# Which queue loads x in the first stage of a graph-convolution kernel: GpSimd's for every row group with known degrees

## The chip, the cores and the metric

The kernel runs on one core of a Trainium2 chip. The metric is the device time of one execution in microseconds; lower is better.

## What is computed

Inputs are `x` (8 x 4096 x 256, float32), `adj` (4096 x 4096, float32, almost all zeros outside a few dense rows and columns) and `W` (256 x 256). The reference, cut to what matters:

```python
HW = einsum('bnf,fo->bno', x, W)
A_norm = relu((adj + adj.T) * 0.5)
D = sum(A_norm, axis=1)
d = where(D > 0, D ** -0.5, 0)
L_norm = eye(N) - d[:, None] * A_norm * d[None, :]
y = relu(einsum('nm,bmo->bno', L_norm, HW))
out = layernorm(x + y, axis=-1)
```

## The kernel before

The work has two stages that follow each other. The first makes the symmetric matrix and the scaled features and puts both into device memory; the second gathers the non-zero parts of the matrix and multiplies.

**First stage.** `adj` is cut into 8 x 8 blocks of 512 x 512. The loop runs over rows of blocks i = 0 to 7 and, in each, over j = i to 7. One step (i, j) does this:

- SP's queue loads block (i, j) and, off the diagonal, block (j, i) (`load_adj`, line 485, 1 MB each, into a pool of 4 buffers).
- `symmetrise`: TensorE transposes one block by pieces of 128 x 128 (line 495), VectorE adds the other block to it into a `sym` tile (line 499, pool of 3 buffers). Off the diagonal both blocks are done, so a step has 32 transposes and 8 additions.
- Work "beside" it: `multiply` (line 564), the product of an already finished row group with the first 128 columns of the matrix (its "strip"), 8 matmuls; and `form` (lines 575 to 624) for one row group m of 128 nodes.
- `keep`: ScalarE halves and clips (line 503), VectorE sums each 32 columns (line 506, into a pool of 3 `sums` buffers), GpSimd marks which sums are positive (`uses`, line 507), VectorE adds up row sums (line 511), and ScalarE's queue stores the tile to `a_dram` (line 512, 1 MB).

After a row of blocks its degrees are complete: GpSimd raises them to the power -1/2 (`r`, line 526), and corrected diagonal blocks are stored to `a_dram` from GpSimd's queue (line 538).

**`form(m, known, alone)`** loads the 8 x 128 x 256 part of x that belongs to row group m, in two halves of 512 KB (`xin`, a pool of 3 buffers), transposes it on TensorE (line 595, 16 pieces; 8 for each half), copies it out with ScalarE (line 596) and multiplies by W (line 606, 32 matmuls). If the degrees of the group are known, ScalarE scales the result (line 616), stores it to `g_dram` (line 621) and calls `fetch(m)`, which loads the strip for the later `multiply`. If they are not, the result is held in on-chip memory and scaled later (`release`); these are the last ten groups, 22 to 31. The groups with known degrees are 0 to 21. Steps with i = 1 to 3 form groups 0 to 11 (and, in row 1, the held groups 30 and 31); steps with i = 4 to 7 form groups 12 to 21.

The two loads of `form` go one of two ways. With `alone` false they are issued on SP's queue (line 588), among the adj loads. With `alone` true they go through `load` (line 554) on GpSimd's queue, where each is placed behind the load issued by `load` before it; the strips go through the same function, so x loads and strips form one sequence there. The call that chooses is line 711.

Each engine executes its instructions in order, and a DMA that waits for its buffer keeps what is behind it on that engine's queue waiting. A scheduler fixes the order on each queue when the program is built. On GpSimd's queue stand, in the first stage, the `uses` operations, the powers `r`, the diagonal copies and stores, the strips, short memsets of constants for the second stage (lines 214, 215 and 221, some 45 after each `uses` up to about 138 us), and the x loads with `alone` true.

**Second stage.** GpSimd issues indirect loads of matrix rows (line 951) and of features (line 959), TensorE multiplies them (line 1166), and ScalarE, VectorE and SP's queue evict, normalise and store.

Of the kernel before, what the change touches and what calls it, by code (L numbers as in the profile page):

```python
# [67 lines left out]
def kernel(  # L68
# [401 lines left out]
    with (  # L470
# [12 lines left out]
        def load_adj(i, j):  # L483
            t = blocks_pool.tile([P, A, S], F32, tag="adj", name=f"adj_{i}_{j}")
            nc.sync.dma_start(
                t,
                adj[i * S : (i + 1) * S, j * S : (j + 1) * S].rearrange("(a p) s -> p a s", p=P),
            )
            return t

        def symmetrise(i, j, tij, tji, sym):
            for a in range(A):
                pt = psum.tile([P, S], F32, tag="b0", name=f"tr_{i}_{j}_{a}")
                for c in range(A):
                    ins = nc.tensor.transpose(  # L495
                        pt[:, c * P : (c + 1) * P], tji[:, c, a * P : (a + 1) * P], ident
                    )
                done_pe.append(ins.ins)
                nc.vector.tensor_add(sym[:, a, :], pt, tij[:, a, :])  # L499
                yield  # L500
# [50 lines left out]
        def load(t, source):  # L551

            with tc.issue_after(loads[-1]) if loads else nullcontext():
                loads.append(nc.gpsimd.dma_start(t, source).ins)

        def fetch(m):

            t = strips.tile([P, P], F32, tag="strip", name=f"strip_{m}")
            load(t, a_dram[m * P : (m + 1) * P, :P])
            return t  # L560

        def multiply(m, g, strip):
            for c in range(G // S):
                nc.tensor.matmul(  # L564
                    lead[c],
                    lhsT=strip,
                    rhs=g[:, c * S : (c + 1) * S],
                    start=not done,
                    stop=len(done) == NB - 1,
                    skip_group_check=True,  # L570
                )
                yield
            done.append(m)

        def form(m, known, alone=False):

            H = B // 2  # L580
            xin = []
            for h in range(2):
                t = xpool.tile([P, H, F], F32, tag="xin", name=f"xin_{m}_{h}", bufs=3)
                source = x[h * H : (h + 1) * H, m * P : (m + 1) * P, :].rearrange("b p f -> p b f")
                if alone:
                    load(t, source)
                else:
                    nc.sync.dma_start(t, source)
                xin.append(t)
            xt = xpool.tile([P, B, FC, P], F32, tag="xt", name=f"xt_{m}", bufs=1)  # L590
            for b in range(0, B, 2):
                pt = psum.tile([P, 2, FC, P], F32, tag="b0", name=f"xtr_{m}_{b}")
                for k in range(2):
                    for c in range(FC):
                        nc.tensor.transpose(pt[:, k, c, :], xin[b // H][:, b % H + k, c * P : (c + 1) * P], ident)  # L595
                nc.scalar.copy(xt[:, b : b + 2], pt)  # L596
                yield
            if known:
                g = xpool.tile([P, G], F32, tag="g", name=f"gt_{m}")
            else:  # L600
                g = hpool[m].tile([P, G], F32, name=f"held_{m}")
            for b in range(0, B, 2):
                pg = psum.tile([P, 2 * FO], F32, tag="b0", name=f"pg_{m}_{b}")
                for k in range(2):
                    for c in range(FC):
                        ins = nc.tensor.matmul(  # L606
                            pg[:, k * FO : (k + 1) * FO],
                            lhsT=xt[:, b + k, c, :],
                            rhs=w_sb[:, c, :],
                            start=(c == 0),  # L610
                            stop=(c == FC - 1),
                        )
                done_pe.append(ins.ins)
                to = g[:, b * FO : (b + 2) * FO]
                if known:
                    nc.scalar.mul(to, pg, r[:, m : m + 1])
                else:
                    nc.scalar.copy(to, pg)
                yield
            if known:  # L620
                nc.scalar.dma_start(g_dram[m * P : (m + 1) * P, :], g)
                waiting.append((m, g, fetch(m)))
            else:
                held[m] = g
# [12 lines left out]
        def release_all(i):  # L637
            for m in range(i * A, (i + 1) * A):
                if m in held:
                    release(m)  # L640
            lower_diagonal(i, diags.pop(i))
# [3 lines left out]
        known, early = [], list(range(NB - HOLD, NB))  # L645

        def quota(i, j):

            if i in (2, 3) and j == i:
                return 0  # L650
            return int(j > i or i > 3)
# [3 lines left out]
        def run_due(flush=False):  # L655
            for d in due:
                d[0] -= 1
            while due and (flush or due[0][0] <= 0):
                _, fn, args = due.pop(0)
                fn(*args)  # L660
# [37 lines left out]
        for i in range(NS):  # L698
            diag = stat1.tile([P, A, P], F32, tag="diag", name=f"diag_{i}")
            for j in range(i, NS):  # L700
                tij = load_adj(i, j)
                tji = load_adj(j, i) if j > i else tij
                parts = [(i, j, tij, tji)] + ([(j, i, tji, tij)] if j > i else [])
                parts = [(p, spool.tile([P, A, S], F32, tag="sym", name=f"sym_{p[0]}_{p[1]}")) for p in parts]
                beside = [multiply(*args) for args in waiting]
                waiting.clear()
                products = len(beside)

                for _ in range(quota(i, j)):
                    if known:  # L710
                        beside.append(form(known.pop(0), True, i >= 4))
                    elif early:
                        beside.append(form(early.pop(0), False))
                for p, sym in parts:
                    for _ in symmetrise(*p, sym):
                        pass
                if i == NS - 1:


                    release_all(i - 1)  # L720
                    beside = beside[products:] + beside[:products]
                for n, b in enumerate(beside):
                    with tc.issue_after(done_pe[-1]) if i == NS - 1 and n < 2 else nullcontext():
                        for _ in b:
                            pass
                for (rows, cols, _, _), sym in parts:
                    keep(rows, cols, sym, diag)
                    run_due()
            degrees(i)
            diags[i] = diag  # L730
            if i != NS - 2:
                release_all(i)
            known += range(i * A, min((i + 1) * A, NB - HOLD))
            if i in (1, 2, 3, 4):
                u = SEQ[i - 1]
                at = 4 if i == 4 else 1
                gap = 2 if i == 1 else 1
                due += [[at, patterns, (u,)], [at + 1, count_place, (u,)]]
                due += [[at + 1 + (k + 1) * gap, more, (u,)] for k in range(3)]
                if i < 4:  # L740
                    due.append([at + 2 + 3 * gap, count_place_rest, (u,)])
            if i in (2, 4):
                u = SEQ[i // 2 - 1]
                at = 4 if i == 2 else 0
                pieces = spread_early(u)
                due += [[at + k, next, (pieces, None)] for k in (1, 2, 3, 3, 4)]
                due.append([at + 5, collect_index, (u,)])
            due.sort(key=lambda d: d[0])
# [579 lines left out]
```

## Time and profile before

| What | us |
|---|---|
| median of 3 runs | 1491.0 (1484.07 to 1491.29) |
| profiled execution, its time | 1490.8 |
| profiled execution, its span | 1488.3 |
| PE busy, of the span | 1381.5 (93%) |
| VectorE busy | 1042.9 (70%) |
| GpSimd busy | 761.4 (51%) |
| ScalarE busy | 360.8 (24%) |

The span runs from the first to the last instruction of the profiled execution; 2.5 us of its time lie around it. In the page's queue list, q1 is SP's queue, q10 is ScalarE's and q0 is GpSimd's:

```profile
q0 software_dynamic: 55200, 282.68, 49.1%
q1 hardware_dynamic: 93472, 126.89, 24.7%
q10 hardware_dynamic: 67872, 130.32, 23.1%
```

The columns are packets, MB, and the time that their packets took as a share of 16 DMA engines over the span. The x loads of the first stage and their neighbours in the list of DMA issues (queue, count, KB each, median us to landing):

```profile
adj<-in_adj_dram SPq DMA_DIRECT2D x64, 1024.0 KB, 10.2
a_dram<-sym ACTq DMA_DIRECT2D x64, 1024.0 KB, 8.9
...
xin<-in_x_dram SPq DMA_DIRECT2D x44, 512.0 KB, 11.9
...
xin<-in_x_dram POOLq DMA_DIRECT2D x20, 512.0 KB
```

A line such as "PE tr L495 <- DVE sym L499: 11.2, 10, 4.0" in the list of waits says that PE's instruction of line 495 was let go by VectorE's of line 499, for 11.2 us in total in 10 cases, of which the longest took 4.0 us. PEld is TensorE's weight load; SPq is SP's queue, which only issues DMAs. The granted clock is the share of full speed at which TensorE was allowed to run. The DMA share is the busy share of the core's 16 DMA engines; as packets overlap, it can stand a little above 1.

### The profile page before, as it was taken

The numbers are of one execution on the slowest core, as the hardware profiler recorded it, in microseconds if no ns is written. First come the engines' busy times: TensorE is split into PE (matmuls) and PEld (weight loads), VectorE is DVE, ScalarE is ACT, GpSimd is POOL, SyncE is SP. The second block draws the span as 40 slices with busy tenths as digits, with TensorE's granted clock in tenths as the row PEclk, the third lists the DMA queues.
The fourth block names the chain that finished last, engine by engine and source line by source line (L and its number), as shares of the span: only waits on it lengthen the run. The fifth ranks groups of instructions, "written<-read, shape, count | busy, mean of one in ns | idle before, by whom it ended". The sixth has DMA issues, their size and how long they took to land.

```text
span 1488.3 us, 29574 instructions
## 1 busy us (share of the span) xinstructions
PE 1381.5 (93%) x10960; PEld 749.5 (50%) x10960; DVE 1042.9 (70%) x3174; ACT 360.8 (24%) x462; POOL 761.4 (51%) x1556
## 2 busy tenths in 40 slices
PE   7998988979998998999999999999989999988993
PEld 6777877756777763343433333333333334433341
DVE  4668569879687763219486897788889029999654
ACT  4555554444544460000101101100100010011111
POOL 2445010010322336765775777777767557777761
PEclk9999999999999999999999999999999999998996
DMA  9999999998999999999999999999999889999994
GB/s 348 364 377 380 403 365 358 387 388 314 357 361 354 368 388 379 390 400 337 370 379 358 375 401 374 382 394 378 348 387 386 312 292 383 370 352 398 393 369 144
DMA packets 216694, 541.85 MB, mean 364 GB/s; under 512 B 19070, under 2 KB 108862, under 8 KB 182110
## 3 DMA queue, kind: packets, MB, share of 16 engines
q0 software_dynamic: 55200, 282.68, 49.1%
q1 hardware_dynamic: 93472, 126.89, 24.7%
q10 hardware_dynamic: 67872, 130.32, 23.1%
q8 instruction: 89, 1.46, 0.4%
q14 instruction: 61, 0.50, 0.1%
HBM read 434.91 MB, written 136.34 MB: 384 GB/s over the span
## 4 chain that ended last, share of the span: by engine, by line
PE 53%; DMA 23%; DVE 16%; issue 5%; ACT 2%; POOL 1%; ACTq 0%; DVEq 0%; POOLq 0%
PE py L1166 33%; PE pg L606 9%; DMA g<-g_dram,gi 7%; DMA a_dram<-sym 6%; DVE sym L499 3%; PE lead L564 3%; PE tr L495 3%; PE xtr L595 3%; DMA xin<-in_x_dram 3%; DMA out_dram<-xr 2%; DMA xr<-in_x_dram 2%; DMA ga<-a_dram,ai 2%; DVE stats L786 2%; DVE xr L810 1%; DVE xr L777 1%
## 5 line engine op out<-in xcount | busy, mean ns | idle before, releaser
L1166 PE MATMUL py<-g,ga 64*32 64x512 f32 (+1 forms) x7072 | 612.4, 610 | 23.1 <-DMA g<-g_dram,gi 22.0
L1166 PEld LDWEIGHTS py<-g,ga 64*32 64x32 f32 (+1 forms) x7072 | 226.8, 114 | 392.1 <-issue 314.7
L959 POOL DMA_INDIRECT g<-g_dram,gi x265 | 297.7, 1124 | 113.6 <-issue 71.0
L951 POOL DMA_INDIRECT ga<-a_dram,ai x265 | 282.9, 1068 | 136.2 <-PE py L1166 64.1
L767 ACT ACTIVATE y<-py,minus_r 128x512 f32<-128x512 f32 x120 | 72.7, 688 | 789.1 <-PE py L1166 634.4
L606 PE MATMUL pg<-w_sb,xt 128*128 128x256 f32 x1024 | 229.7, 383 | 4.2 <-ACT xt L596 4.2
L1166 PE MATMUL py<-g_hub,gh 128*128 128x512 f32 x496 | 229.2, 604 | 3.8 <-DVE pos_k L239 3.8
L606 PEld LDWEIGHTS pg<-w_sb,xt 128*128 128x128 f32 x1024 | 194.8, 193 | 30.5 <-ACT xt L596 5.0
L499 DVE TENSOR_TENSOR sym<-tr,adj 128x512 f32<-128x512 f32 x256 | 162.8, 683 | 57.4 <-PE tr L495 40.6
L506 DVE TENSOR_REDUCE sums<-sym 128x64 f32<-128x2048 f32 x64 | 145.3, 2279 | 62.4 <-ACT sym L503 62.4
L1166 PEld LDWEIGHTS py<-g_hub,gh 128*128 128x128 f32 x496 | 91.2, 191 | 136.3 <-issue 123.5
L495 PE MATMUL tr<-ident,adj 128*128 128x128 f32 x1024 | 135.9, 280 | 21.4 <-DVE sym L499 14.8
L503 ACT ACTIVATE sym<-sym 128x2048 f32<-128x2048 f32 x64 | 122.6, 1915 | 113.6 <-DVE sym L499 101.2
L507 POOL TENSOR_SCALAR uses<-sums 128x64 uint8<-128x64 f32 x64 | 24.8, 388 | 239.5 <-DVE sums L506 203.5
L442 DVE TENSOR_SCALAR low<-lists 128x17 f32<-128x17 f32 (+8 forms) x14 | 2.5, 175 | 200.0 <-PE lists L430 200.0
L495 PEld LDWEIGHTS tr<-ident,adj 128*128 128x128 f32 x1024 | 115.2, 143 | 53.7 <-DVE sym L499 32.5
L777 DVE TENSOR_TENSOR xr<-xr,y 128x2048 f32<-128x2048 f32 x31 | 70.9, 2286 | 54.7 <-ACT y L767 42.0
L595 PE MATMUL xtr<-ident,xin 128*128 128x128 f32 x512 | 72.8, 291 | 21.3 <-DVE sym L499 12.3
L810 DVE TENSOR_SCALAR xr<-xr,mv,root 128x256 f32<-128x256 f32 x248 | 87.6, 425 | 1.1
L786 DVE BATCH_NORM_STATS2 stats<-xr 128x6 f32<-128x256 f32 x248 | 84.1, 412 | 1.1
L564 PE MATMUL lead<-gt,strip 128*128 128x512 f32 x176 | 83.2, 593 | 0.0
L596 ACT COPY xt<-xtr 128x512 f32<-128x512 f32 x128 | 68.0, 592 | 60.0 <-PE xtr L595 58.6
(157 smaller groups left out, 1057.7 us busy)
## 6 DMA issues: line engine op xcount, KB each, us to landing
adj<-in_adj_dram SPq DMA_DIRECT2D x64, 1024.0 KB, 10.2
a_dram<-sym ACTq DMA_DIRECT2D x64, 1024.0 KB, 8.9
out_dram<-xr SPq DMA_DIRECT2D x31, 1024.0 KB, 23.6
xr<-in_x_dram ACTq DMA_DIRECT2D x28, 1024.0 KB, 15.1
xin<-in_x_dram SPq DMA_DIRECT2D x44, 512.0 KB, 11.9
g_dram<-gt ACTq DMA_DIRECT2D x22, 1024.0 KB, 8.9
xin<-in_x_dram POOLq DMA_DIRECT2D x20, 512.0 KB
g_dram<-held ACTq DMA_DIRECT2D x10, 1024.0 KB, 14.1
```

What stands on the lines that cost most here:

```text
L495: ins = nc.tensor.transpose(pt[:, c * P : (c + 1) * P], tji[:, c, a * P : (a + 1) * P], ident)
L499: nc.vector.tensor_add(sym[:, a, :], pt, tij[:, a, :])
L503: nc.scalar.activation(sym, sym, AF.Relu, scale=0.5)
L506: nc.vector.tensor_reduce(sums, sym.rearrange("p a (c q) -> p a c q", q=E), AX.X, ALU.add)
L564: nc.tensor.matmul(lead[c], lhsT=strip, rhs=g[:, c * S : (c + 1) * S], start=not done, stop=len(done) == NB - 1, skip_group_check=True,)
L595: nc.tensor.transpose(pt[:, k, c, :], xin[b // H][:, b % H + k, c * P : (c + 1) * P], ident)
L606: ins = nc.tensor.matmul(pg[:, k * FO : (k + 1) * FO], lhsT=xt[:, b + k, c, :], rhs=w_sb[:, c, :], start=(c == 0), stop=(c == FC - 1),)
L786: nc.vector.bn_stats(stats[:, b, :], z[:, b, :])
L810: nc.vector.tensor_scalar(z[:, b, :], z[:, b, :], mv[:, b, 0:1], rstd[:, b : b + 1], ALU.subtract, ALU.mult,)
L951: nc.gpsimd.indirect_dma_start(out=at if both else at[:, : E if one else P], out_offset=None, in_=a_pairs if both else a_groups if one els ...
L959: nc.gpsimd.indirect_dma_start(out=gt, out_offset=None, in_=g_dram, in_offset=bass.IndirectOffsetOnAxis(ap=gi[:, t : t + 1], axis=0), boun ...
L1166: return nc.tensor.matmul(py[2 * u + 1 + b][c][cols, :], lhsT=at[ps, off + cols.start : off + cols.stop], rhs=gt[ps, c * S : (c + 1) * S], ...
```

## The change

```diff
@@ -708,7 +708,7 @@
                 for _ in range(quota(i, j)):
                     if known:
-                        beside.append(form(known.pop(0), True, i >= 4))
+                        beside.append(form(known.pop(0), True, True))
                     elif early:
                         beside.append(form(early.pop(0), False))
```

For groups 0 to 11 the two loads of `form` move from SP's queue (line 588) to GpSimd's (line 554). `form`'s loads and `load`, which the edit leaves as they are:

```python
        def load(t, source):

            with tc.issue_after(loads[-1]) if loads else nullcontext():
                loads.append(nc.gpsimd.dma_start(t, source).ins)
...
                if alone:
                    load(t, source)
                else:
                    nc.sync.dma_start(t, source)
```

In the order that is built, TensorE's, VectorE's and ScalarE's instructions stand as before. SP's queue has 24 instructions fewer and GpSimd's 24 more; every other instruction stays on its queue. On GpSimd's queue the strips of groups 1 to 11 also change place, since each now follows its own group's x loads in the sequence of `load`. The ten held groups still load x on SP's queue.

## The prediction

> **What bounds the kernel now.** I read the sums by stage first, then who waits for whom in the stage that the change touches, then SP's own waits, then the two kinds of x load. The columns of the first view are start:end, length, busy us (x instructions) of PE, PEld, DVE, ACT and POOL, granted clock, DMA share, GB/s.
>
> ```profile
> 0.00:105.00 105.00, 92.63 (x541) 77.70 (x542) 62.23 (x95) 55.13 (x69) 37.98 (x609) 1.00 1.01 360
> 105.00:350.00 245.00, 220.39 (x1234) 177.15 (x1232) 186.59 (x343) 119.51 (x137) 40.71 (x245) 0.97 1.02 378
> 350.00:545.00 195.00, 184.84 (x1028) 143.48 (x1029) 149.30 (x358) 97.70 (x116) 53.78 (x94) 0.99 0.96 354
> ```
>
> The first stage lasts until about 550 us. Rows of blocks i = 1 to 3, whose x loads move, lie in the second line. Two resources are near their end there at once: TensorE is busy 220.4 of 245 us, and the DMA engines are full (share 1.02). The third line is rows 4 to 7, where x already comes on POOL's queue: DMA share 0.96, PE 95% busy. Thus the whole stretch of the change has 24.6 us of idle PE, and no more than that can be won in it, a few slow-clock microseconds apart. In the same 245 us (waiter, releaser: us, times, longest):
>
> ```profile
> PE tr L495 <- DVE sym L499: 11.2, 10, 4.0
> PE tr L495 <- DMA adj<-in_adj_dram: 5.8, 1, 5.8
> PE xtr L595 <- DVE sym L499: 4.8, 3, 2.1
> PE xtr L595 <- DMA xin<-in_x_dram: 2.2, 1, 2.2
> DVE sym L499 <- DMA a_dram<-sym: 1.7, 2, 1.2
> ```
>
> PE waits for x itself once, 2.2 us; for adj once, 5.8 us; the rest is VectorE, whose order the change leaves alone. SP's queue in the same stretch:
>
> ```profile
> SPq L485 <- DVE sym L499: 139.0, 18, 13.5
> SPq L588 <- PE xtr L595: 24.6, 19, 3.1
> SPq L588 <- PE pg L606: 10.6, 5, 4.1
> ```
>
> SP stands 35.2 us in front of an x load that waits for its buffer, with adj loads behind it, but 139 us in front of adj loads that wait for their own buffers. The two kinds of x load, from the views of lines 588 and 554:
>
> ```profile
> L588 SPq DMA_DIRECT2D xin<-in_x_dram x44: 367/401/4616, 0.8 to 354.3; - x44
> DMA to landing us min/median/max: 7.4/11.9/18.2
> ...
> L554 POOL DMA_DIRECT2D xin<-in_x_dram x20: 748/802/837, 355.9 to 528.2; - x20
> ```
>
> On SP's queue half a row group takes 11.9 us from issue to landing. The page has no landing for POOL's loads; in the trace's packets of queue 0 their last packet ends 5.5 to 9.3 us after the issue, median 7.4.
>
> [...] The trace gives the packets: x on SP moves in 1,024 B packets (mean 48 ns), on POOL in 4,096 B packets (mean 176 ns), adj and a_dram in 2,048 B packets (median 84 ns). [...] five stretches of 3.4 us at 0.5 lie between 105 and 390 us, each beside an idle PE, and each costs 3.4 x 0.5 = 1.7 us of PE work.
>
> **The change part by part.** 12 row groups (m = 0 to 11), 24 loads of 512 KB, 12.6 MB.
>
> 1. *SP loses 24 issues* of 0.4 us, about 10 us of a queue that mostly waits: nothing. Its 35 us of waits in front of x go, all but those of the held groups 30 and 31, whose loads stay on SP. What the adj loads behind gain: step (1,5)'s second adj left at 148.9 us, 1.0 us after the x load ahead of it, but was first needed at 171. The one adj load that PE waited for, (3,4)'s second, left at 297.8, when (2,7)'s last addition freed its buffer at 297.7; no x load was then waiting before it. Value 0, bounds 0 and -1.7 (a slow-clock window).
>
> 2. *POOL gains 24 issues* of 0.80 us = 19 us, on an engine busy 40.7 of 245 us, and in order. Behind a waiting x load stand `uses` (L507, which frees one of three sums buffers for VectorE), `r` (L526) and the diagonal stores (L538). I followed each load in the new order. A second half waits for the first eight transposes of the group before, a first half for its last eight; the `uses` behind it belongs to the same step and in this trace runs later (steps 3,4 and 3,5: last transpose ends at 319.6 and 336.6, `uses` at 320.4 and 338.1). So what is added is at most the issue, 0.8 us, with two sums buffers to spare: 0. Only early in i = 1 is POOL late: group 1's first half leaves after four diagonal stores, at about 126.6 instead of 113.4 us, and its second after two sets of memsets, about 135 instead of 132.2. Transposed at 146.8 and 147.7; 135 + 7.4 = 142.4: hidden, with 5 us to spare.
>
> 3. *The strip loads (L554)* are chained behind x. Ten went out close together at 126 to 135 us; all but the first now follow the second half of their group's x. They take 4 to 7 us to the last packet and are first read by the lead products one step (15.7 us) later: 0. Seven strip issues fewer and one x load more ahead of the `uses` at 130.3 us let it run about 3 us sooner; no engine is listed as waiting for it: 0.
>
> 4. *The DMA time of x.* 512 packets x 48 ns / 16 = 1.53 us a load become 128 x 176 ns / 16 = 1.40 us: 0.126 us, and 24 loads make 3.0 us of full DMA. Where the DMA is what runs out that comes off the path, elsewhere it doesn't. Bounds 0 and -3; I take -2.
>
> 5. *The x stall.* At 197.2 PE waited 2.2 us for the second half of held group 30 (it stays on SP; issued at 179.9, 17.1 us to land) and the clock fell, 1.7 us more: 3.9 us. Groups 2 and 3 no longer stand in SP's ring before it; the adj loads do. Bounds 0 and -3.9; I take -2.
>
> 6. *The turns.* [...] Stores (median 8.9 us to landing) free the sym buffers. The chain of waits passes through only three of them in this stretch (10.3, 10.0 and 8.4 us): 0 to +4.2; I take +1.
>
> Sum: 0 + 0 + 0 - 2 - 2 + 1 = -3 us. The profiled execution is 1490.8 us (span 1488.3 and 2.5 around it), 0.2 under the median of 1491.0 us. 1490.8 - 3 = 1487.8: I say 1488. The later stages have the same instructions in the same order and only start sooner. If the covers of 2 fail, what is late next is the second half of x: slack before was 3.6 us (group 2: landed 159.8, read 163.4).
>
> **The rivals.**
>
> *A. DMA is the true limit of these rows.* Then faster x and a lighter SP ring take away all DMA-ended stalls with their slow clock: x 2.2 + 1.7, adj 5.8 + 1.7, and the two store waits 1.7, together 13.1 us: 1490.8 - 13.1 = 1477.7. For it: share 1.02, and adj landings of median 7.6 us in rows 4 to 7 against 10 to 11 here. Against it: PE's own work in a full step is 3.7 (tr) + 3.4 (lead) + 1.7 (xtr) + 6.9 (pg) = 15.7 us in the chain's pieces, and eight steps between 105 and 350 us already take 15.2 to 16.3 from first transpose to first transpose.
>
> *B. Stores lose their turn (slower).* In rows 4 to 7, where x has its own queue:
>
> ```profile
> DVE sym L499 <- DMA a_dram<-sym: 9.6, 3, 5.9
> ```
>
> That is 9.6 us of VectorE over 10 groups, against 1.7 between 105 and 350 us. Place: the addition of the next block, which cannot write its sym tile. Price: about 1 us a group, 12 groups, 12 us: 1503. It decides once a store lands more than about 2 us later than now. Against it: the median store landing is no longer there (8.9 us) than here (9.1 to 9.9), and PE itself lost only 2.0 us behind the 5.9 us one.
>
> *C. POOL holds up `uses`.* If some waits in the real order fall badly, one step stalls by up to its 3.4 us and a slow-clock window: +3 to +5, 1495.
>
> *D. Nothing moves the end:* 1491, inside the likeliest case's range.
>
> **How the numbers follow.** 0.5% of 1491 is 7.5 us, about what a measurement of this kernel can tell from no change (its three runs lie 7.2 us apart). Forecast with D 0.44, A 0.29, B 0.21, C 0.06. A counts as faster save where only part of it comes; B as slower; C mostly as the same. Faster 0.30, same 0.47, slower 0.23. The likeliest case alone: 1482 to 1495, by adding the ends of 1 and 4 to 6 (-8.6 and +4.2). For 8 in 10 the range reaches to A and most of B: 1477 to 1501.
>
> **What would show it.** Right: x on POOL lands in 7 to 9 us with no PE wait for xin from known groups; packets of 4,096 B; SP's L588 waits between 105 and 350 us shrink from 35 to under 12 us; the steps still 15.7 us; the first stage within 8 us of now. Step 5: the wait at 197 us shorter than 2 us. Wrong: the DVE and ACT sym rows waiting for a_dram over 8 us in rows 1 to 3 (B); POOL's x loads or `uses` ending VectorE's sums waits (C); adj stalls gone and the share under 1.0 (A). A change in the second stage's length would be outside all of this.

## The result, and the profile after

| | before | after |
|---|---|---|
| median of 12 runs, us | 1488.95 (1484.07 to 1491.52) | 1493.76 (1491.27 to 1499.84) |
| profiled execution, us (span) | 1490.8 (1488.3) | 1494.0 (1491.9) |
| PE busy, us | 1381.5 | 1384.3 |

The ratio after/before is 1.0045, 95% interval [1.0031, 1.0058]: slower by 0.45%, some 6.7 us of 1489 (the two medians alone are 4.8 us apart). The forecast was 0.2% faster. The time lies inside the range given, but the sign is wrong and the difference is larger than its uncertainty.

The sums by stage of the kernel after, columns as in the view of before:

```profile
0.00:105.00 105.00, 92.48 (x539) 77.41 (x540) 63.02 (x95) 54.86 (x68) 38.95 (x610) 1.00 1.01 362
105.00:350.00 245.00, 221.93 (x1225) 180.69 (x1224) 184.73 (x336) 120.18 (x138) 57.21 (x266) 0.94 1.01 372
350.00:545.00 195.00, 183.78 (x1024) 141.02 (x1023) 150.74 (x365) 95.03 (x113) 54.37 (x93) 0.99 0.96 355
```

In the line of the change (105 to 350 us) PE is busy for 1.5 us more than before and at a lower clock, 0.94 against 0.97. The DMA engines are as full (1.01) and move less, 372 against 378 GB/s. So PE isn't idle for longer in this stretch; it works more slowly.

Who waits for whom in the same 245 us (waiter, releaser: us, times, longest):

```profile
POOL xin L554 <- PE xtr L595: 65.1, 12, 12.5
...
PE tr L495 <- DVE sym L499: 12.1, 10, 4.0
...
ACT sym L503 <- DMA a_dram<-sym: 4.6, 1, 4.6
...
PE tr L495 <- DVE deg L523: 4.2, 1, 4.2
...
DVE sym L499 <- DMA a_dram<-sym: 4.0, 2, 2.0
...
PE xtr L595 <- DMA xin<-in_x_dram: 0.3, 1, 0.3
```

The waits for loads have nearly gone, as hoped: PE's wait for x fell from 2.2 to 0.3 us, and its 5.8 us for adj became a 4.2 us wait whose last releaser is a small VectorE operation. In their place stand waits for stores: VectorE and ScalarE now wait 4.0 + 4.6 = 8.6 us for `a_dram<-sym`, against 1.7 before. ScalarE's part says little, though: it is one wait at 126 us, and the unchanged order alone (s1_before below) has one of 6.1 us at 350 us in the same view. SP's own queue in the same stretch:

```profile
SPq L485 <- DVE sym L499: 190.1, 28, 15.3
SPq L485 <- PE tr L495: 14.9, 14, 2.1
...
SPq L588 <- PE xtr L595: 3.7, 3, 3.0
...
SPq L588 <- PE pg L606: 1.2, 1, 1.2
```

SP's waits in front of x shrank from 35.2 to 4.9 us, and it merely stands longer in front of adj loads (190 us against 139), which wait for their own buffers. The list of DMA issues:

```profile
adj<-in_adj_dram SPq DMA_DIRECT2D x64, 1024.0 KB, 9.8
a_dram<-sym ACTq DMA_DIRECT2D x64, 1024.0 KB, 9.9
...
xin<-in_x_dram POOLq DMA_DIRECT2D x44, 512.0 KB
...
xin<-in_x_dram SPq DMA_DIRECT2D x20, 512.0 KB, 11.3
```

By this list an adj load lands 0.4 us sooner than before (9.8 against 10.2) and a store 1.0 us later (9.9 against 8.9). But it matches only some of the issues with a landing, 37 and 31 of the 64 stores. The trace holds 16 completion signals for each load and store; from the issue to the 16th, over all 64, the median of the adj loads is 10.1 us both times, and that of the stores is 10.2 against 9.6. Landings below are counted in this way.

**One store, followed.** Three engines of the kernel after in step (2,6); the columns are start, length, engine and operation, and in brackets the idle time before it and its releaser. First ScalarE's queue, then GpSimd, then VectorE:

```profile
271.21 0.37 ACTq L512 DMA_DIRECT2D a_dram<-sym  x1
```

```profile
270.54 0.81 POOL L554 DMA_DIRECT2D xin<-in_x_dram  x1 [9.23 <-PE xtr L595]
271.38 0.38 POOL L507 TENSOR_SCALAR uses<-sums 128x64 uint8<-128x64 f32 x1
...
272.31 0.75 POOL L554 DMA_DIRECT2D xin<-in_x_dram  x1
```

```profile
282.99 2.48 DVE L499 TENSOR_TENSOR sym<-tr,adj 128x512 f32<-128x512 f32 x4 [1.92 <-DMA a_dram<-sym]
```

A store of 1 MB leaves at 271.2, between two x loads of 512 KB. Its last completion signal comes at 282.9, 11.7 us later, and VectorE, which wants that sym buffer, stands still for 1.92 us until 282.99. In the kernel before, the store of the same block took 9.9 us (270.6 to 280.5) and let no addition wait. Over the ten stores of row 2's blocks off the diagonal the mean is 9.92 us before and 11.53 after, and four of the ten take 2.7 to 3.6 us longer.

The prediction counted three stores in the chain of work that ended last between 105 and 350 us, of 10.3, 10.0 and 8.4 us. In the kernel after there are four (start, length), and the second is the one just followed:

```profile
114.05 10.23 DMA a_dram<-sym
...
271.21 11.66 DMA a_dram<-sym
...
302.14 10.55 DMA a_dram<-sym
...
340.12 9.97 DMA a_dram<-sym
```

In the second profile of this kernel (e5_all below) the store at 271 us is on the chain too; in s1_before, the unchanged order, it isn't.

**Where the clock went.** The same 30 us at the start of row 3 (steps (3,3) and (3,4)), before and then after; the eighth number, behind POOL's, is the granted clock:

```profile
303.00:313.00 10.00, 4.37 (x25) 3.99 (x26) 8.51 (x20) 1.91 (x1) 3.62 (x7) 0.83 1.05 405
313.00:323.00 10.00, 7.80 (x38) 6.44 (x39) 7.57 (x9) 4.73 (x6) 2.14 (x7) 0.83 0.99 350
323.00:333.00 10.00, 10.00 (x51) 7.27 (x50) 6.75 (x13) 3.75 (x4) 0.37 (x1) 1.00 1.06 391
```

```profile
303.00:313.00 10.00, 4.53 (x25) 3.92 (x22) 7.40 (x14) 2.91 (x2) 1.78 (x3) 0.70 1.03 371
313.00:323.00 10.00, 7.49 (x33) 6.68 (x34) 10.00 (x15) 3.67 (x4) 4.88 (x11) 0.50 0.87 314
323.00:333.00 10.00, 10.00 (x47) 8.09 (x47) 3.82 (x6) 5.03 (x6) 1.63 (x4) 0.95 1.01 371
```

PE is busy 22.2 us of 30 before and 22.0 after, yet from 313 to 323 us the clock is 0.83 before and 0.50 after. PE's order of time there, before and then after, shows why:

```profile
307.86 3.68 PE L495 MATMUL tr<-ident,adj 128*128 128x128 f32 x20 [5.78 <-DMA adj<-in_adj_dram]
312.30 1.25 PE L495 MATMUL tr<-ident,adj 128*128 128x128 f32 x8 [0.77 <-DVE sym L499]
315.69 0.66 PE L495 MATMUL tr<-ident,adj 128*128 128x128 f32 x4 [2.13 <-DVE sym L499]
```

```profile
301.98 1.91 PE L495 MATMUL tr<-ident,adj 128*128 128x128 f32 x16
308.06 3.64 PE L495 MATMUL tr<-ident,adj 128*128 128x128 f32 x16 [4.17 <-DVE deg L523]
313.56 1.11 PE L495 MATMUL tr<-ident,adj 128*128 128x128 f32 x4 [1.86 <-DVE sym L499]
315.21 1.97 PE L495 MATMUL tr<-ident,adj 128*128 128x128 f32 x8 [0.53 <-DVE sym L499]
318.59 1.11 PE L495 MATMUL tr<-ident,adj 128*128 128x128 f32 x4 [1.42 <-DVE sym L499]
```

The idle time is 5.78 + 0.77 + 2.13 = 8.7 us before and 4.17 + 1.86 + 0.53 + 1.42 = 8.0 us after. But after it is spread over more gaps. The one of 1.86 us comes from VectorE, and that from a store:

```profile
312.81 0.69 DVE L499 TENSOR_TENSOR sym<-tr,adj 128x512 f32<-128x512 f32 x1 [2.04 <-DMA a_dram<-sym]
```

In the clock's records of before, two separate windows of 3.4 us at half speed lie here (from 307.1 and 317.4); after, one unbroken stretch of 17.1 us (from 307.0). In the view of after, 16 transposes take 1.91 us just before that stretch (301.98) and 3.64 us in it (308.06). PE was busy for 6.1 of the 6.8 us and for 12.2 of the 17.1, so by estimate (12.2 - 6.1) x 0.5 = 3.0 us more of its work was lost.

### The profile page after: what moved, and what is told of

It is laid out like the page before. It is cut to its first block, busy times and chain, and to the rows that moved or that the text cites. A ratio compares the mean times of both kernels' runs of the same rounds, so it can differ in the third digit from the quotient of the medians.

```text
span 1491.9 us, 29571 instructions
## 1 busy us (share of the span) xinstructions
PE 1384.3 (93%) x10960; PEld 755.0 (51%) x10960; DVE 1045.2 (70%) x3174; ACT 361.3 (24%) x462; POOL 785.4 (53%) x1580
## 4 chain that ended last, share of the span: by engine, by line
PE 52%; DMA 24%; DVE 15%; issue 4%; ACT 2%; POOL 2%; DVEq 0%; ACTq 0%; POOLq 0%
PE py L1166 35%; PE pg L606 8%; DMA a_dram<-sym 8%; DMA g<-g_dram,gi 6%; DVE sym L499 4%; DMA xr<-in_x_dram 3%; PE xtr L595 3%; PE tr L495 3%; PE lead L564 3%; DMA out_dram<-xr 2%; DMA xin<-in_x_dram 2%; DVE xr L810 1%; DVE stats L786 1%; DMA ga<-a_dram,ai 1%; ACT sym L503 1%
## 5 line engine op out<-in xcount | busy, mean ns | idle before, releaser
L951 POOL DMA_INDIRECT ga<-a_dram,ai x265 | 288.1, 1087 | 134.5 <-PE py L1166 64.8
L495 PE MATMUL tr<-ident,adj 128*128 128x128 f32 x1024 | 139.8, 285 | 23.1 <-DVE sym L499 18.1
L495 PEld LDWEIGHTS tr<-ident,adj 128*128 128x128 f32 x1024 | 119.1, 146 | 55.9 <-DVE sym L499 35.5
L554 POOL DMA_DIRECT2D xin<-in_x_dram x44 | 35.1, 797 | 179.6 <-PE xtr L595 175.5
L595 PE MATMUL xtr<-ident,xin 128*128 128x128 f32 x512 | 73.7, 293 | 18.4 <-DVE sym L499 12.0
```

The lines of the kernel that those rows point to most:

```text
L495: ins = nc.tensor.transpose(pt[:, c * P : (c + 1) * P], tji[:, c, a * P : (a + 1) * P], ident)
L951: nc.gpsimd.indirect_dma_start(out=at if both else at[:, : E if one else P], out_offset=None, in_=a_pairs if both else a_groups if one els ...
```

## The experiments

The theory of the turns, which the expectations name after part 6 of the prediction, is the guess that x loads on GpSimd's queue make the stores to `a_dram` land later. Step times below are from the first transpose of a step to the first of the next. They are from single profiles. The medians of whole kernels are of 14 or 22 runs (51 and 67 for the kernel before), those of the first stage alone of 5. An interval is that of the ratio to the kernel before on the same chip.

**Rows alone, and no row at all.** Line 711 chooses; each kernel changes only its last argument.

```diff
-                        beside.append(form(known.pop(0), True, i >= 4))
+                        beside.append(form(known.pop(0), True, i == 1 or i >= 4))   # e1_row1
+                        beside.append(form(known.pop(0), True, i == 2 or i >= 4))   # e2_row2
+                        beside.append(form(known.pop(0), True, i >= 3))             # e3_row3
+                        beside.append(form(known.pop(0), True, False))              # e4_none
```

Row 1 (groups 0 to 3):

> Only the groups formed in row 1 of blocks (0 to 3) move to GpSimd's queue; rows 2 and 3 stay on SP. Theory of the turns [...]: the loss of 4.8 us is spread by loads, so about a third of it, +1.6 us, less the stall of 2.2 us plus 1.7 us of slow clock that went away in step (1,6), so -2 to +1. Theory of the order (GpSimd's in-order queue is late, and it is busiest with memsets in row 1): most of the loss is here, +3 to +5. Theory of one place (the long slow-clock stretch at the start of row 3): 0 or a gain of up to 4.

Row 2 (groups 4 to 7):

> Only the groups formed in row 2 of blocks (4 to 7) move. Theory of the turns: +1.5 to +3, with a store near 271 us landing in 11 to 12 us and VectorE waiting for it. Theory of the order: near 0, since GpSimd has little to do there. Theory of one place: if the delay of 1.8 us that reaches row 3 brings about the long slow-clock stretch, +4 to +5 and that stretch of 10 us or more near 307 us is seen; else 0.

Row 3 (groups 8 to 11):

> Only the groups formed in row 3 of blocks (8 to 11) move. Theory of the turns: +1.5 to +3. Theory of the order: near 0. Theory of one place: +4 to +5 if the loads of row 3 themselves make the slow-clock stretch near 307 us, 0 if it is row 2.

No group at all on GpSimd's queue:

> All 22 groups load x on SP's queue, rows 4 to 7 too. Theory of the turns: each group costs 4.8/12 = 0.4 us on GpSimd's queue, so the ten of rows 4 to 7 give back 4 us: about 1485. Theory of the order and theory of one place: nothing known for rows 4 to 7, where SP would now wait for x buffers in front of adj loads: between 0 and +5.

| kernel | median us | ratio to before |
|---|---|---|
| before, same chip | 1488.61 | 1 |
| e1_row1 | 1489.35 | 1.0007 [0.9993, 1.0021] |
| e2_row2 | 1488.46 | 0.9999 [0.9982, 1.0016] |
| e3_row3 | 1488.27 | 1.0003 [0.9990, 1.0016] |
| e4_none | 1482.95 | 0.9968 [0.9954, 0.9982] |

No single row explains the loss; each alone is within 0.2% of before. The other direction is clear: with the x loads of all 22 groups on SP's queue the kernel is 0.32% faster than before, although PE then does wait for x (9.3 us in one case, at the end of the first stage). This is the best of all versions run whole.

**The change again, and pairs of rows.**

```diff
-                        beside.append(form(known.pop(0), True, i >= 4))
+                        beside.append(form(known.pop(0), True, True))      # e5_all
+                        beside.append(form(known.pop(0), True, i != 3))    # e6_row12
+                        beside.append(form(known.pop(0), True, i >= 2))    # e7_row23
+                        beside.append(form(known.pop(0), True, i != 2))    # e8_row13
```

> The changed kernel itself once more, beside its pairs of rows. All theories: ratio 1.003 to 1.006, as first measured (1.0045). Below 1.002 the first loss was partly chance. A second profile tells whether the 17 us of slow clock at the start of row 3 belongs to this kernel (then 10 us or more again near 307 us) or to one execution.

> Rows 1 and 2 on GpSimd's queue, row 3 on SP. If each row adds its share (theory of the turns): about two thirds of the loss, +3 to +4.5 us, though the single rows came out at +1.0, -0.1 and +0.4 us. If the loss needs neighbouring rows (a delay in one row that the next can no longer hide): here and in rows 2 and 3 together +3 or more, and none in rows 1 and 3.

> Rows 2 and 3 on GpSimd's queue, row 1 on SP. Theory of the turns with shares that add up: +3 to +4.5 us. Neighbouring rows: +3 or more. One place, the slow-clock stretch at the start of row 3, which needs a late row 2 and loads in row 3: nearly the whole loss, +5 to +7, with 10 us or more of slow clock near 307 us.

> Rows 1 and 3 on GpSimd's queue, row 2 on SP. Theory of the turns with shares that add up: +3 to +4.5 us. Neighbouring rows: 0 to +1.5. One place at the start of row 3: 0 to +2.

| kernel | median us | ratio to before |
|---|---|---|
| before, same chip | 1488.34 | 1 |
| e5_all | 1493.94 | 1.0044 [1.0031, 1.0057] |
| e6_row12 | 1489.48 | 1.0014 [1.0001, 1.0027] |
| e7_row23 | 1490.05 | 1.0009 [0.9994, 1.0024] |
| e8_row13 | 1489.24 | 1.0006 [0.9992, 1.0019] |

The loss repeats on a second chip. The pairs cost 0.06 to 0.14%, and no two of them add up to the 0.44% of all three. The medians of whole runs therefore don't say which row costs what; the profiles do by place.

**By place.** All versions; those whose names begin with s or t hold the first stage alone and are described further down. The columns: rows whose x came on GpSimd's queue; mean time to landing of the ten stores of row 2's blocks off the diagonal; length of step (2,6); length of steps (3,3) and (3,4) together; half-clock time between 303 and 330 us.

| kernel | rows on GpSimd's queue | store, us | (2,6), us | (3,3)+(3,4), us | half clock, us |
|---|---|---|---|---|---|
| before | 4-7 | 9.92 | 15.8 | 28.0 | 6.8 |
| e4_none | none | 10.02 | 15.8 | 28.5 | 10.2 |
| e1_row1 | 1, 4-7 | 9.77 | 15.8 | 28.3 | 6.8 |
| e3_row3 | 3-7 | 10.24 | 16.0 | 28.8 | 13.7 |
| e8_row13 | 1, 3-7 | 10.53 | 15.8 | 29.8 | 13.7 |
| e2_row2 | 2, 4-7 | 11.73 | 17.8 | 27.8 | 10.2 |
| e6_row12 | 1, 2, 4-7 | 11.34 | 17.5 | 28.8 | 10.2 |
| e7_row23 | 2-7 | 12.15 | 17.9 | 29.8 | 17.1 |
| after | 1-7 | 11.53 | 17.1 | 29.6 | 17.1 |
| e5_all | 1-7 | 11.35 | 16.4 | 30.3 | 17.1 |
| s1_before | 4-7 | 9.77 | 15.8 | 28.1 | 6.8 |
| s1_none | none | 9.96 | 15.8 | 27.3 | 6.8 |
| s1_row23 | 2-7 | 11.31 | 16.9 | 28.7 | 13.7 |
| s1_after | 1-7 | 11.52 | 17.2 | 30.1 | 13.7 |
| t_before | 4-7 | 9.66 | 15.8 | 28.0 | 6.8 |
| t_strips | 1-7 | 11.31 | 16.7 | 28.4 | 10.2 |
| t_token | 4-7 (order of 1-7) | 9.91 | 15.8 | 28.4 | 6.8 |
| t_token_all | none (order of 1-7) | 10.02 | 15.8 | 26.9 | 6.8 |
| t2_row23 | 2-7 | 11.16 | 16.3 | 28.7 | 13.7 |
| t2_token23 | 4-7 (order of 2-7) | 9.84 | 15.8 | 28.0 | 6.8 |

In the nine kernels with row 2's x on GpSimd's queue its stores take 11.2 to 12.2 us and step (2,6) 16.3 to 17.9; in the eleven others 9.7 to 10.5 and 15.8 to 16.0. The start of row 3 is less clean. In the nine with row 3's x on GpSimd's queue it takes 28.4 to 30.3 us, with 10.2 to 17.1 us of half clock; in the others 26.9 to 28.8, with 6.8 to 10.2. So the ranges touch, and row 3's own stores hardly land later (9.5 to 9.8 us on the mean against 9.1 to 9.8). In row 1 no effect stands out of the scatter: steps (1,2) and (1,3) together take 33.3 to 34.2 us with row 1 on GpSimd's queue and 31.8 to 33.4 without.

**The first stage alone.** The twelve whole runs of the kernel before spread over 7.5 us, which hides differences of a few us. These kernels end after the first stage.

```diff
+    nc.scalar.copy(ident, lead[0][:, :P])
+    nc.sync.dma_start(out[0, :P, :P], ident)
+    return
+
```

> The first stage alone: the second stage, the fallback and all stores of the result are left out (one 128x128 piece is stored at the end), with the order of the first stage on every queue as in the kernel before. All theories: about 590 us; it is the base for the next three.

> The first stage alone (the rest left out as above), all 22 known groups on GpSimd's queue. If the loss of 5.6 us lies in the first stage (turns, order, slow clock): 4 to 7 us above the first stage of the kernel before. If it comes in the second stage from when the first one ends: within 1.5 us.

> The first stage alone (the rest left out as above), all groups on SP's queue. Turns: 3 to 6 us below the first stage of the kernel before, as the whole kernel was. If the gain came in the second stage: within 1.5 us.

> The first stage alone (the rest left out as above), rows 2 and 3 on GpSimd's queue, row 1 on SP. If the shares of the rows add up in the first stage and the second stage hides part of them: 3 to 4.5 us above the first stage of the kernel before, although the whole kernel was only 1 to 2 us slower. If all three rows are needed for the loss: within 1.5 us.

| kernel | median us | lowest to highest |
|---|---|---|
| s1_before | 587.02 | 586.64 to 588.93 |
| s1_after | 589.95 | 589.09 to 591.81 |
| s1_none | 581.43 | 580.23 to 583.10 |
| s1_row23 | 589.81 | 589.34 to 592.66 |

Some 2.9 us of the loss lie in the first stage (the five runs of each just don't overlap), and rows 2 and 3 by themselves show as much (2.8). With the x loads of all 22 groups on SP's queue the stage is 5.6 us shorter than before. Beside these kernels and those of the next two series, the median listed for the whole kernel before is 1739 to 1742 us, at a granted clock of 0.92, instead of 1488 us at 0.97. I don't know why; the first-stage kernels are compared only with each other.

**Order or bytes?** The change moves two things: the bytes, and where they stand in GpSimd's order. t_token keeps GpSimd's order of the changed kernel but puts a short memset of half the x buffer where the load was, for groups 0 to 11, and brings the bytes over SP's queue; t_token_all does so for all 22 groups. t_strips is the changed kernel with the strips in a sequence of their own, early again.

```diff
-                if alone:
+                if alone == 2:
+                    with tc.issue_after(loads[-1]) if loads else nullcontext():
+                        loads.append(nc.gpsimd.memset(t[:, :2, :], 0.0).ins)
+                    nc.sync.dma_start(t, source)
+                elif alone:
...
-            load(t, a_dram[m * P : (m + 1) * P, :P])
+            with tc.issue_after(strip_loads[-1]) if strip_loads else nullcontext():
+                strip_loads.append(nc.gpsimd.dma_start(t, a_dram[m * P : (m + 1) * P, :P]).ins)
```

The first five added lines are t_token's and t_token_all's, the last two t_strips'. The first stage of the kernel before, on this chip:

> The first stage alone, as in the kernel before (the second stage, the fallback and the stores of the result are left out). All theories: 586 to 588 us; base for the next three on the same chip.

> The first stage alone (the rest left out). GpSimd stands in exactly the order of the changed kernel, but for groups 0 to 11 each x load there is a memset of half the xin buffer, which waits for the same buffer; the load itself follows on SP's queue, in SP's order of the kernel before. Turns: as the first stage of the kernel before or up to 1 us above it. Order: 2.5 to 4 us above it, as with the loads on GpSimd's queue.

> As the last, but for all 22 groups: GpSimd waits as in the changed kernel, and all x goes over SP's queue. Turns: near the 581.4 us of all x on SP's queue, 5 to 6 us below the base. Order: near 590, 3 us above the base.

> The first stage alone (the rest left out). All 22 groups load x on GpSimd's queue, but the strips have a chain of their own and go out early again, ten close together near 126 us. Turns or order: 2.5 to 4 us above the base, as with the strips behind x. The strips' move as the cause: within 1 us of the base.

| kernel | median us | lowest to highest |
|---|---|---|
| t_before | 587.22 | 584.78 to 589.24 |
| t_token | 589.61 | 587.94 to 591.49 |
| t_token_all | 585.51 | 582.12 to 588.60 |
| t_strips | 588.81 | 586.83 to 592.95 |

t_token didn't give a clean answer. By place it shows none of the losses of rows 2 and 3 (table above), but its median is 2.4 us above the base, about what the theory of the order expected. SP's waits from 105 to 370 us suggest a fault of the experiment itself: SP stood behind late GpSimd work. t_token_all, with the same fault, is 1.7 us below the base with overlapping runs, which fits neither theory's number.

```profile
SPq L588 <- POOL xin L587: 46.2, 17, 17.0
...
SPq L588 <- POOL uses L507: 15.8, 5, 12.8
```

t_strips lies between the base and the changed kernel, and its runs overlap with both: the strips' move is neither shown to cost anything nor shown to be free. The last pair leaves row 1 alone, and puts memsets (t2_token23) against loads (t2_row23) in rows 2 and 3, on one chip:

```diff
-                        beside.append(form(known.pop(0), True, i >= 4))
+                        beside.append(form(known.pop(0), True, i >= 2))                                # t2_row23
+                        beside.append(form(known.pop(0), True, 2 if i in (2, 3) else int(i >= 4)))     # t2_token23
```

> The first stage alone, as in the earlier run of the same kernel: the second stage, the fallback and the output stores are left out. Groups 4 to 11 (rows 2 and 3) load x on GpSimd's queue, groups 0 to 3 on SP's. All theories: 589 to 590.5 us, as before (589.8), 2 to 3 us above the first stage of the kernel before (587.0 and 587.2); from 313 to 323 us the granted clock is near 0.5 (0.50 in its earlier profile) and step (2,6) is about 1 us longer. If it falls under 588, the loss was within what one chip and one job scatter.

> The first stage alone; second stage, fallback and output stores are left out. For groups 4 to 11 GpSimd has a short memset of the x buffer where the changed kernel has a load, chained as that load is, so GpSimd's order is that of rows 2 and 3 on GpSimd, but the bytes come over SP's queue, in 1,024 B packets; groups 0 to 3 are as in the kernel before, so SP doesn't wait for GpSimd in row 1. Theory of the turns (the packets of GpSimd's queue delay the stores): 586 to 588, with a store's mean landing in row 2 near 8.9 us, no loss at step (2,6) and two short windows of half clock at 303 to 323 us (mean there 0.83). Theory of the order on GpSimd's queue: 589 to 590.5 as the kernel beside it, with the loss at steps (2,6) and (3,4).

| kernel | median us | lowest to highest |
|---|---|---|
| t2_row23 | 591.54 | 588.21 to 593.44 |
| t2_token23 | 583.92 | 581.50 to 586.83 |

With the same order on GpSimd's queue, the bytes on SP's make the stage 7.6 us shorter; the runs don't overlap. That is more than the 2.8 us between s1_row23 and s1_before. Part of it may be chance: the kernel before wasn't run beside this pair, t2_token23 is also below the bases of the other two chips, and t2_row23's profile, that of its slowest run, has 20.5 us more half clock before 303 us. The windows of t2_row23 and then of t2_token23, at the start of row 3:

```profile
313.00:323.00 10.00, 6.38 (x28) 5.17 (x28) 7.96 (x17) 3.73 (x2) 4.27 (x10) 0.50 0.97 374
```

```profile
313.00:323.00 10.00, 10.00 (x47) 8.67 (x45) 4.31 (x6) 6.67 (x9) 1.98 (x4) 0.83 0.97 336
```

As the theory of the turns expected: clock 0.50 with the bytes on GpSimd's queue, 0.83 with GpSimd's order alone. Step (2,6) is 16.3 against 15.8 us, and the mean store of row 2 lands after 11.16 against 9.84 us. What costs time in rows 2 and 3 is thus where the bytes go, not the order on GpSimd's queue. The memset kernel also puts the loads back into SP's order, at other moments; and no run changes the size of the packets alone. So it isn't shown whether the stores are late because of the packets' size, the separate queue, or the moment at which the loads leave.

**The same thing further on.** e4_none, s1_none and t_token_all share one trait: groups 12 to 21 don't load x on GpSimd's queue either. At the first step of row 4 the kernel before has this on PE:

```profile
384.41 1.88 PE L564 MATMUL lead<-gt,strip 128*128 128x512 f32 x4
388.05 0.66 PE L595 MATMUL xtr<-ident,xin 128*128 128x128 f32 x4 [1.75 <-DVE sym L499]
```

and e4_none this:

```profile
385.55 1.88 PE L564 MATMUL lead<-gt,strip 128*128 128x512 f32 x4
387.34 0.66 PE L595 MATMUL xtr<-ident,xin 128*128 128x128 f32 x4
```

PE waits 1.75 us for an addition in the one and not at all in the other. The addition itself begins when the store of block (3,7) has landed, at 387.2 us before; that store takes 13.8 us before and 11.9 in e4_none. Over all profiles it takes 12.8 to 14.0 us where rows 4 to 7 use GpSimd's queue and 10.6 to 11.9 where they don't. PE waits 0.7 to 2.0 us at this place in all seventeen profiles whose rows 4 to 7 use GpSimd's queue, and in none of the three where the bytes come on SP's. t_token_all has GpSimd's order of the changed kernel, so here too it is the bytes. Step (4,4) takes 13.9 to 14.9 us in those three and 15.7 to 18.4 in the others.

## Why the prediction was wrong

The step that failed is part 6, "The turns". It named an effect that the runs bear out, stores that land later, and mis-sized it at +1 us within 0 to +4.2. The +4.2 is 1.4 us for each of three stores, and these 1.4 us were the author's estimate, which no trace of the kernel before shows. The part took over the three stores of the chain before, and priced the wait without the clock. Beside it, parts 4 and 5 booked 4 us of gains that didn't come; without them even +1 would have had the right sign. What the runs showed in place of part 6:

- The stores of row 2 land later by 1.6 us on the mean (11.53 against 9.92), near the estimated 1.4. But a fourth store joins the chain, the one of 11.7 us that VectorE waits for in step (2,6), and that step grows by 1.3 us.
- What was left out is the clock. The prediction priced slow-clock windows in the gains (1.7 us each) and none in the cost of the turns. After the change the half clock between 303 and 330 us lasts 17.1 us instead of 6.8, some 3.0 us of PE's work. (3,3) and (3,4) together are 1.6 us longer: (3,3) is 1.6 us shorter, (3,4) 3.2 us longer.
- By places, the changed profile loses 1.5 us in (1,2) and (1,3), 1.9 in (2,5) and (2,6), 1.6 in (3,3) and (3,4), 1.3 in (3,6) and (3,7): 6.3 us. The 1.3 of (2,6) follows the queue of the bytes in every experiment, the 1.6 of (3,3) and (3,4) in most. The 1.5 of row 1 is within scatter (s1_before has 33.4 us there, as much as the kernel after), and for the rest the same cause is only argued. The profile's own difference is 3.2 us: among other things, the kernel before was 3.6 us longer in (1,6) and 1.9 in (4,4).

The other parts:

1. *SP loses 24 issues: 0.* SP's waits in front of x went from 35.2 to 4.9 us (under 12 was forecast). adj loads issued from 105 to 375 us took 10.3 instead of 10.6 us on the mean to landing. This bought no time that the medians show.
2. *POOL in order: 0.* Held. No wait of VectorE for a `uses` appears among the waits of rows 1 to 3, and t2_token23, which has this order in rows 2 and 3, has no loss.
3. *Strips: 0.* Not settled (t_strips).
4. *DMA time: -2.* The packets are as forecast, 4,096 B and 166 ns on the mean between 230 and 300 us, and x on GpSimd's queue lands in 7.3 to 11.2 us, median 8.8, against 12.2 on SP's queue before. The expected 2 us don't show in any median. The likely reason is that shorter packet time in sum is no gain when the store that is waited for lands later; this is argued.
5. *The x stall at 197 us: -2.* It went (step (1,6) is 3.6 us shorter in the profile of after), but it was an accident of one execution: it is missing as well in the profiles of e2_row2, e3_row3 and s1_before, whose rows up to there load x as the kernel before does. It was in the profile, not in the median, and its loss is no gain.
6. See above.

So of -3 us the -4 of parts 4 and 5 was not there. If the others are taken at 0, some +6.7 is left for part 6; its two places above make 2.9 us, as much as the first stage alone shows, and the rest isn't located. Rival B (stores land later, 1503) is nearest to what happened, at about half its price: at most 6.7 us over 12 groups, 0.56 us a group instead of 1. Its sign (waits for `a_dram` over 8 us) was met by 8.6, but s1_before, with nothing changed, has 1.9 + 6.1 = 8.0, so the sign doesn't tell the two apart. Rival A fell: the load-side waits went and the time rose. Rival C fell with part 2. The argument against B, that the median store lands no later in rows 4 to 7, was the error of judgement. There too it is single stores that cost, as that of (3,7), behind which PE waited 1.75 us, and e4_none is 0.32% faster without those rows' loads on GpSimd's queue.

The prediction also read its slow-clock windows too kindly. All five are 3.4 us long, but only two of them (from 232.0 and 307.1 us) follow a long idle gap (4.0 and 5.8 us); in front of the others no single gap is longer than 2.2 us.

In the profile of before the half-clock windows start at 197.9, 232.0, 307.1, 317.4 and 389.1 us, all whole multiples of 3.41 us apart, and the remainder of such a start by 3.41 is another in other profiles (3.4 before, 3.2 after, 2.3 in e3_row3). Whether this is one reason why single profiles scatter by a few us isn't shown.

**Open.** Why one or two rows cost at most 0.14% in whole runs when all three cost 0.44%: by place, the versions with rows 2 or 3 show losses of 0.8 to 2.1 us each in their profiles. Why the first stage alone shows 2.9 us of the loss while whole runs show 4.8 to 6.7. The spans of the second stage, from its first matmul (line 1166) to the end, are 905.9 us before, 906.2 after and 905.1 in e5_all, so these profiles don't show the remainder there. But with the same instructions they are 901.1 to 903.5 us in the six versions with one or two rows, and 895.6 in e4_none, whose first stage ends some 7 us later than before (589.6 against 582.5, after the wait of 9.3 us) and which is still faster. So the second stage varies by more than the loss from profile to profile, and it may take up part of what the first one loses; no run settles this. And how much of the 7.6 us between t2_row23 and t2_token23 is chance of that chip's five runs.

## What to carry to other kernels

In this kernel faster loads of x (8.8 us to landing instead of 12.2) were worth nothing where the store beside them (11.7 us instead of 9.9 in step (2,6)) was what a buffer waited for. With the DMA engines full (a share of 1.01 and 1.02 here), ask whose transfer will land later, and price that delay at the buffer it frees: a store that wasn't on the chain before can join it. Price a new short wait on a busy TensorE with the clock, as one does the gains: here waits of 0.5 to 1.9 us lay within 17.1 us of half clock, where there had been 6.8. And look for a stall in a second execution, or for a reason why it must recur, before booking its removal.

## What the runs showed of the hardware

About the same idle time came with very different clocks. 8.7 us of idle PE within 14 us, with one gap of 5.78 us, went with two windows of 3.4 us at half clock; 8.0 us as 4.17, 1.86, 0.53 and 1.42 us went with 17.1 us without a break. Behind the first gap, the half clock lasted through gaps of only 0.5 to 1.9 us, and in the profile of before three of five half-clock windows followed gaps of at most 2.2 us. What decides isn't shown.

One x load of 512 KB costs its issuer 0.80 us on GpSimd's queue and 0.40 on SP's, and its packets are 4,096 B there and 1,024 B here. With another issuing engine more changed than the time of the issue: SP's waits in front of x fell from 35.2 to 4.9 us, x landed sooner (8.8 against 12.2 us), row 2's stores later (11.5 against 9.9), and the whole became 0.45% slower.
